# Moving the products of the next key projection ahead of the mixing, a value tile into the second step and half a broadcast one block later, in a two-layer attention kernel

## The chip, the cores and the metric

The kernel runs on one core of one Trainium2 chip. The metric is the device time of one execution in microseconds (us). The kernel before takes 3994.44 us, the median of three runs (3994.28 to 3995.66). All times in this document that carry two decimals and no other mark are read from one profiled execution of the kernel before.

## The reference, cut to what matters

The input x is 8 images of 512 channels and 32 x 32 positions (1024 tokens), in float32. Layer 0 is a group-normalised attention with a projection. Layer 1, where the change lies, is this, for each image, on y, the group-normalised output of layer 0:

```python
q = einsum('oc,bct->bot', w_q, y)      # the same for k and v, 8 heads of 64
attn = einsum('bhdq,bhdT->bhqT', q, k) * scale
attn = einsum('gh,bhqT->bgqT', w_head, attn)     # heads are mixed ahead of the softmax
attn = softmax(attn, axis=-1)
attn = (attn - mean) / sqrt(var + EPS) * gamma + beta   # mean, var over a whole head
out = einsum('bhqT,bhdT->bhqd', attn, v).reshape(b, t, c)
out = out @ w_proj.T + b_proj
```

The result is x plus the output of each layer.

## The kernel before

The engines' instructions stand in the order in which the Python code writes them, engine by engine; a step that is written later is behind all earlier ones on its own engine, and nothing but data and free buffers holds one engine back for another.

Layer 1 goes through the images b = 0 to 7. The queries of an image are cut into eight blocks p = 0 to 7 of 128 queries (NT = 8). A block's work goes through a pipeline of three iterations of p, so the loop has nine iterations p = 0 to 8, each of four steps t = 0 to 3, all in `Attention1.step` (L1852):

- **scores** (L1622, matmul L1629): eight products of keys and queries per block; each goes to a tile of two PSUM banks and is copied to SBUF as `raw`, by ScalarE at L1641 (in the first block every other one by VectorE, L1639).
- **regroup** (L1643, DMA L1647): `raw` is laid out anew by sixteen DMAs of 256 KB per block from SyncE's queue into `re_t`, so that the 8 heads of a query lie in one group of partitions.
- **mix** (L1657, matmul L1666): four mixings of the heads per block, one iteration behind the scores, 32 small matmuls each, into two PSUM tiles; ScalarE takes the exponentials (L1679).
- **flip** (L1687, transpose L1694) and **moments** (L1699, L1708) on VectorE, right behind each mixing.
- **values** (L1712, L1724): attention times v, two iterations behind the scores; ScalarE copies the sums out (**leave**, L1740).
- **totals** (L1756): every second block, three tiny matmuls give the softmax sums of two blocks; their reciprocals go through HBM (four DMAs `zd<-rz`, L1772) and come back spread over the partitions in two DMAs of 256 KB, `rzb<-zd`, L1778. **divide** (L1803) multiplies them into the result, on GpSimd for the first three pairs of blocks. Both the DMAs and the multiplication stand in GpSimd's queue; for the last pair it is SyncE's queue and VectorE.

PSUM tiles of scores, mixings and projections share one pool, `ps_m`, of three buffers of two banks each (L1278, `m_psum`).

An `Agenda` (L28) holds further work under slot numbers; `ag.run(slot)` writes it at that point. `ag.run(4 * p + t)` stands at the end of each step, and some half slots within it. The work in it that matters here:

- `v_pair(b, i)` (L1448): 16 matmuls (L1456) make two of the eight tiles of v; ScalarE copies the first (L1460), VectorE the second (L1461). Pairs 0 and 1 are made between the images, pairs 2 and 3 in slots 1 and 3, that is in the iteration p = 0.
- The key projection of the next image, a `Projection` (L1358) by Strassen-like products in the order 1, 6, 2, 7, 5, 3, 4. `k_go(m)` writes the eight matmuls of product m (L1381) and puts its evacuation on a list, which `k_leave()` (L1443) writes out. Products 1, 2, 6 and 7 have the slots 31.5, 32.5, 33.5 and 34.5, that is the iteration p = 8, which has no scores any more. Product 1 is copied by ScalarE (L1390); product 2 adds to the same bank and is copied by ScalarE (L1435); 6 and 7 are added into partial sums by VectorE (L1396, L1398). `right_y` (L1426, subtractions L1356) makes the right-hand factors on VectorE in slots 32 and 33.
- Loads of the next image and of weights, from SyncE's queue.

In the step, the half slots stand behind the mixing of the step, and `k_leave()` behind those:

```python
                    if old:
                        self.mix(p - 1, 0)
                    ag.run(4 * p - 0.5)
```

Of the kernel before, what the change touches and what calls it, by code (L numbers as in the profile page):

```python
# [467 lines left out]
def tile_two_attention_layers(  # L468
# [19 lines left out]
    nc = tc.nc  # L488
    B, C, T = x_d.shape
    H = w_head.shape[0]  # L490
    D = C // H
# [207 lines left out]
    with ExitStack() as l0:  # L699
# [487 lines left out]
        first = Agenda()  # L1187
# [81 lines left out]
    with ExitStack() as l1:  # L1269
# [15 lines left out]
        def m_psum(nm):  # L1285
            return ps_m.tile([P, 2, FB], F32, tag="m", name=nm)
# [156 lines left out]
        def k_leave():  # L1443
            for fn in due:
                fn()
            due.clear()

        def v_pair(b, i):  # L1448

            if i == 0:  # L1450
                v_t[b] = shared.tile([P, NT, C], F32, tag="v", name=f"v1_{b}")
            ps = m_psum(f"pv1_{b}_{i}")
            w = w_t["v", b]
            for m in range(2):
                for c in range(NCC):
                    nc.tensor.matmul(  # L1456
                        ps[:, m], y_t[b][:, c, ts(2 * i + m, P)], w[:, c],
                        start=(c == 0), stop=(c == NCC - 1),
                    )
            nc.scalar.copy(v_t[b][:, 2 * i], ps[:, 0])  # L1460
            nc.vector.tensor_copy(v_t[b][:, 2 * i + 1], ps[:, 1])  # L1461

        vs = const_tile("vs", [P, H, B])

# [150 lines left out]
        class Attention1:  # L1615
# [140 lines left out]
            def totals(self, n):  # L1756

                b, last = self.b, n == NCH - 1
                bn = self.stats(n)
                del self.bn[n]  # L1760
                ps = acc_psum(f"z1_{b}_{n}")
                nc.tensor.matmul(ps[:64, :32], bn[:, :, 1], sel256, start=True, stop=True)
                for i, x in enumerate((bn[:, :, 2], self.sq)):
                    nc.tensor.matmul(ps[:64, 32:64], x, sel, start=(i == 0), stop=(i == 1))
                rz = stat.tile([64, 32], F32, tag="rz", name=f"rz1_{b}_{n}")
                nc.vector.reciprocal(rz, ps[:64, :32])  # L1766
                nc.vector.tensor_copy(self.zs[:, n], ps[:64, :64])
                zd = dram.tile([2, H, P], F32, tag=f"zd_{b}_{n}", name=f"zd_{b}_{n}")
                queue = nc.sync if last else nc.gpsimd
                for r in range(2):  # L1770
                    for t in range(2):
                        queue.dma_start(  # L1772
                            out=zd[t].rearrange("g (r c q) -> r c g q", r=2, q=4)[r],
                            in_=rz[32 * t + r : 32 * t + 32 : 2].rearrange("c (g q) -> c g q", q=4),
                        )
                self.rzb = zpool.tile([P, T], F32, tag="rzb", name=f"rzb_{b}_{n}")
                for t in range(2):
                    queue.dma_start(  # L1778
                        out=self.rzb[t * D : t * D + D],
                        in_=zd[t].rearrange("g i -> (g i)").partition_broadcast(D),  # L1780
                    )

            def check(self):

# [67 lines left out]
            def step(self, p, t, ag):  # L1852

                new, old, older = p < NT, p >= 1, p >= 2
                if t == 0:
                    if new:
                        for i in range(3):
                            self.scores(p, i)
                    if older:
                        self.values(p - 2, 0, 2, 3)  # L1860
                        self.leave(p - 2, 0)
                        if p % 2:
                            self.sums(p // 2 - 1)
                        if p % 2 == 0 and p >= 4:
                            self.divide(p // 2 - 2, nc.gpsimd)
                    if old:
                        self.mix(p - 1, 0)
                    ag.run(4 * p - 0.5)
                elif t == 1:
                    if older:  # L1870
                        self.values(p - 2, 1, 0)
                        self.flip(p - 1, 0)
                        if p % 2:
                            self.totals(p // 2 - 1)
                        self.moments(p - 1, 0)
                    if new:
                        self.scores(p, 3)
                    if old:
                        self.mix(p - 1, 1)
                    ag.run(4 * p + 0.5)  # L1880
                elif t == 2:
                    if older:
                        self.values(p - 2, 1, 1)
                    if new:
                        self.scores(p, 4)
                        self.scores(p, 5)
                    if old and not new:
                        self.mix(p - 1, 2)
                    ag.run(4 * p + 1.5)
                    if older:  # L1890
                        self.values(p - 2, 1, 2, 3)
                        self.leave(p - 2, 1)
                    if old and new:
                        self.mix(p - 1, 2)
                else:
                    if new:
                        self.scores(p, 6)
                        if old:
                            self.values(p - 1, 0, 0)
                        self.scores(p, 7)  # L1900
                        if old:
                            self.mix(p - 1, 3)
                            self.values(p - 1, 0, 1)
                    else:
                        self.mix(p - 1, 3)
                        self.values(p - 1, 0, 0, 1)
                    ag.run(4 * p + 2.5)
                k_leave()
                if p == 1 or old and t:
                    self.flip(p - 1, t)  # L1910
                    self.moments(p - 1, t)
                if new:
                    for kh, s in (
                        (), ((0, 0), (0, 1), (0, 2)), ((0, 3),), ((1, 0), (1, 1), (1, 2), (1, 3)),
                    )[t]:
                        self.regroup(p, kh, s)
                if old and t == 0:
                    self.piece()
                ag.run(4 * p + t)
# [8 lines left out]
        NV = NT // 4  # L1928
        for b in range(B):
            more = b + 1 < B  # L1930
            a = Attention1(b)
            ag = Agenda()
            for i in range(NV):
                ag.at(1 + 2 * i, lambda i=i: v_pair(b, NV + i))
            if b == 0:
                stages = group_stages(B - 1, B, small_psum1)
                for i in range(3):
# [35 lines left out]
            if not more:  # L1973
                a.values(last, 0, 2, 3)
                a.leave(last, 0)
                a.values(last, 1, 0, 1, 2, 3)
                a.leave(last, 1)
                a.totals(NCH - 1)
                a.instance()
                out1_last(a)  # L1980
                continue
# [4 lines left out]
            a.values(last, 1, 0, 1, 2, 3)  # L1986
            a.leave(last, 1)
            a.totals(NCH - 1)
            a.instance()
            k_leave()  # L1990
            k_go(4, 3)
# [84 lines left out]
```

## Time and profile before

| | us |
|---|---|
| median of three runs | 3994.44 |
| the profiled execution | 3994.71 |
| its span, first to last instruction | 3992.9 |
| TensorE busy with matmuls | 3888.9 |
| VectorE busy | 2772.4 |
| ScalarE busy | 1974.3 |
| GpSimd busy | 141.1 |
| mean granted TensorE clock | 0.994 |

Layer 1 starts at about 1800 us of the span; an image takes about 277 us of it (the first scores of two consecutive images start at 3474.51 and 3751.61).

How to read the lines: PE is TensorE's matmuls, PEld its weight loads, DVE VectorE, ACT ScalarE, POOL GpSimd, SP SyncE. A line of the timeline has start, duration (us), engine, source line, operation, what it writes and reads, shapes, and how many instructions were merged; in brackets is how long the engine sat idle just before, and what ended that. A line of the view of waits has who waited for whom, then the total in us, how often, and the longest. A line of the table by stretches has the stretch, its length, each engine's busy time, and at the end the granted clock of TensorE, the DMA engines' busy share and GB/s.

### The profile page before, as it was taken

Reading aid. Unit: us, or ns where it says so; the run is one execution under the profiler, and the core shown is the slowest. Engines: PE = TensorE matmul, PEld = TensorE weight load, DVE = VectorE, ACT = ScalarE, POOL = GpSimd, SP = SyncE. Lnnn points to the kernel's source line nnn. Section 1 sums busy time; section 2 is a strip of 40 time slices with the busy share of each in tenths; the row PEclk is TensorE's granted clock in tenths of the full one; section 3 lists DMA queues with packets and bytes.
Section 4 is the critical chain, followed back from the end, with each engine's and each line's share of the span. In section 5 each row is a group of like instructions: output and inputs, shape, how many; then the busy total and the mean of one; then the engine's idle time right before and its main releaser. Section 6 shows DMA issues by size and latency. Waiting matters only on the chain. (4 is left out here: it accounts for less than half of the span.)

```text
span 3992.9 us, 95453 instructions
## 1 busy us (share of the span) xinstructions
PE 3888.9 (97%) x41868; PEld 1827.5 (46%) x41868; DVE 2772.4 (69%) x3741; ACT 1974.3 (49%) x2431; POOL 141.1 (4%) x182
## 2 busy tenths in 40 slices
PE   8999999999999999999999999999999999999997
PEld 4353535344343535344544545545444445445354
DVE  4748475766657584856958859859768678588596
ACT  1726363544536271615717628438257166175284
POOL 0000000000000000000100101001001001000010
PEclk9999999999999999999999999999999999999999
DMA  3313131111121221217829749659469287396494
GB/s 121 120 48 117 46 120 48 59 62 67 52 83 57 72 68 58 78 67 186 229 86 229 187 119 242 176 130 232 148 164 229 103 210 205 102 231 183 122 224 122
DMA packets 249593, 519.09 MB, mean 130 GB/s; under 512 B 51024, under 2 KB 58192, under 8 KB 242512
## 3 DMA queue, kind: packets, MB, share of 16 engines
q1 hardware_dynamic: 241984, 500.08, 43.9%
q0 software_dynamic: 7184, 12.81, 1.6%
q8 instruction: 331, 5.42, 0.6%
q14 instruction: 94, 0.77, 0.1%
HBM read 197.16 MB, written 46.92 MB: 61 GB/s over the span
## 5 line engine op out<-in xcount | busy, mean ns | idle before, releaser
L1694 DVE STREAM_TRANSPOSE et<-e 128x2048 f32<-128x2048 f32 x256 | 589.8, 2304 | 155.8 <-ACT e L1679 148.6
L1724 PEld LDWEIGHTS a<-et,v 128*64 128x64 f32 x16384 | 508.0, 138 | 296.2 <-issue 273.2
L1708 DVE BATCH_NORM_STATS2 bn<-e 128x6 f32<-128x512 f32 x1024 | 635.0, 682 | 0.0
L1091 ACT ACTIVATE e<-s 128x1024 f32<-128x1024 f32 x512 | 497.9, 1028 | 233.5 <-PE s L1086 232.2
L1679 ACT ACTIVATE e<-m 128x1024 f32<-128x1024 f32 x512 | 496.9, 1023 | 149.7 <-PE m L1666 51.4
L1724 PE MATMUL a<-et,v 128*64 128x64 f32 x16384 | 555.8, 224 | 13.1 <-DVE et L1694 10.4
L1641 ACT COPY raw<-s 128x1024 f32<-128x1024 f32 x480 | 470.8, 1020 | 183.3 <-PE s L1629 164.5
L1099 DVE TENSOR_TENSOR zacc<-zacc,e 128x1024 f32<-128x1024 f32 x384 | 468.8, 1221 | 84.5 <-ACT e L1091 62.4
L1629 PE MATMUL s<-k,q 64*64 64x512 f32 x4096 | 512.9, 605 | 6.3 <-DVE q L1495 3.1
L1086 PE MATMUL s<-q,k 64*64 64x512 f32 x4096 | 490.1, 593 | 2.3 <-ACT e L1091 2.3
L1112 PE MATMUL a<-e,v 64*64 64x512 f32 x4096 | 484.1, 589 | 0.0
L1666 PE MATMUL m<-re,wmix 32*32 32x512 f32 x8192 | 324.0, 610 | 43.8 <-DMA re<-raw 40.3
L1112 PEld LDWEIGHTS a<-e,v 64*64 64x64 f32 x4096 | 156.7, 133 | 282.8 <-issue 282.2
L1086 PEld LDWEIGHTS s<-q,k 64*64 64x64 f32 x4096 | 147.9, 133 | 275.2 <-issue 240.7
L1629 PEld LDWEIGHTS s<-k,q 64*64 64x64 f32 x4096 | 127.3, 132 | 220.1 <-issue 77.0
L1456 PE MATMUL pv<-wv,y 128*128 128x512 f32 x480 | 212.1, 597 | 0.0
L1740 ACT COPY q<-a 64x256 f32<-64x256 f32 x256 | 94.3, 368 | 190.4 <-PE a L1724 188.7
L1772 POOL DMA_DIRECT2D zd<-rz x96 | 52.5, 552 | 3537.2 <-DVE rz L1766 3535.1
L1666 PEld LDWEIGHTS m<-re,wmix 32*32 32x32 f32 x8192 | 70.8, 103 | 174.2 <-ACT raw L1641 68.6
L1456 PEld LDWEIGHTS pv<-wv,y 128*128 128x128 f32 x480 | 89.3, 190 | 116.9 <-issue 110.3
L1460 ACT COPY v<-pv 128x512 f32<-128x512 f32 x30 | 17.6, 587 | 220.2 <-PE pv L1456 220.2
L1097 DVE TENSOR_TENSOR zacc<-e,e 128x1024 f32<-128x1024 f32 x64 | 78.3, 1224 | 55.5 <-ACT e L1091 55.5
(317 smaller groups left out, 3884.3 us busy)
## 6 DMA issues: line engine op xcount, KB each, us to landing
re<-raw SPq DMA_DIRECT2D x1024, 256.0 KB
left_q<-left_q SPq DMA_DIRECT2D x17, 1792.0 KB
left_p<-left_p SPq DMA_DIRECT2D x17, 1792.0 KB
left_k<-left_k SPq DMA_DIRECT2D x10, 1792.0 KB
x<-in_x_dram SPq DMA_DIRECT2D x32, 512.0 KB
rzb<-zd SPq DMA_DIRECT2D x128, 128.0 KB
x<-x SPq DMA_DIRECT2D x64, 256.0 KB
y<-x SPq DMA_DIRECT2D x32, 512.0 KB
```

Source lines behind the costliest of these rows:

```text
L1086: nc.tensor.matmul(ps[c * D : c * D + D, m], k[r, hp, k0 : k0 + D], q[r, hp, ts(f, FB)], start=True, stop=True,)
L1091: nc.scalar.activation(e[i], ps, AF.Exp, scale=S0 * S0)
L1099: nc.vector.tensor_add(zacc[g], zacc[g], e[i])
L1112: nc.tensor.matmul(acc[g][a][m * D : m * D + D], v[rows, kc, ts(2 * hp + m, D)], e[i][rows, m], start=(kc == 0), stop=(kc == NG - 1),)
L1456: nc.tensor.matmul(ps[:, m], y_t[b][:, c, ts(2 * i + m, P)], w[:, c], start=(c == 0), stop=(c == NCC - 1),)
L1629: nc.tensor.matmul(ps[c * D : c * D + D, m], qo_t[b][r, p, hp, ts(c, D)], k_t[b][r, hp, ts(kh, FB)], start=True, stop=True,)
L1641: nc.scalar.copy(dst, ps)
L1666: nc.tensor.matmul(ps[a // 2][c * 32 : c * 32 + 32, a % 2].rearrange("p (r h k) -> p h r k", r=2, h=2), wmix[rows].rearrange("p g i -> p ( ...
L1679: nc.scalar.activation(e[:, :, 2 * h : 2 * h + 2].rearrange("p r a k -> p a r k"), ps[h].rearrange("p a (r k) -> p a r k", r=2), AF.Exp,)
L1694: nc.vector.transpose(self.et[p, u].rearrange("p kb (r st a) g q -> p st kb r (a g q)", r=2, st=2)[:, st], self.e[p, s].rearrange("p r a ( ...
L1708: nc.vector.bn_stats(self.bn[n][:, p % 2, s, a], e[:, :, a].rearrange("p r k -> p k r"))
L1724: nc.tensor.matmul(acc[two * D : two * D + D, s].rearrange("p (x q) -> p x q", q=4), v_t[b][:, kb, ts(g, D)], et[:, kb, :, g], start=(kb = ...
```

## The change

Six edits, all in layer 1:

1. In every step the half slots, and now `k_leave()` with them, are written ahead of the step's mixing. So each of the products 1, 2, 6 and 7 of the next key projection, and its evacuation, stands ahead of mixing 0, 1, 2 and 3 of the iteration p = 8.
2. A new half slot `4 * p - 0.25` stands behind mixing 0.
3. `v_pair` takes the halves to make. Pair 3 is made in two parts: its first tile in slot 3, as before, its second tile in slot 3.75, that is behind mixing 0 of the iteration p = 1 and ahead of the VectorE work of that step. Each part has a PSUM tile of its own.
4. `broadcast(t)` issues one of the two DMAs `rzb<-zd`. `totals` calls the first; the second is written in step 1 of the next iteration (for the last pair: right behind `totals`).
5. The multiplication on GpSimd, `divide`, moves from step 0 to the end of step 3 of the same iteration.
6. In the first block, all four regroupings of the first half of the keys are written in step 1; before, the fourth was in step 2.

```diff
-        def v_pair(b, i):
+        def v_pair(b, i, ms=range(2)):
...
-            for m in range(2):
+            for m in ms:
...
-            nc.scalar.copy(v_t[b][:, 2 * i], ps[:, 0])
-            nc.vector.tensor_copy(v_t[b][:, 2 * i + 1], ps[:, 1])
+            for m in ms:
+                copy = nc.vector.tensor_copy if m else nc.scalar.copy
+                copy(v_t[b][:, 2 * i + m], ps[:, m])
...
-                for t in range(2):
-                    queue.dma_start(
-                        out=self.rzb[t * D : t * D + D],
-                        in_=zd[t].rearrange("g i -> (g i)").partition_broadcast(D),
-                    )
+                self.zd, self.zq = zd, queue
+                self.broadcast(0)
+
+            def broadcast(self, t):
+
+                self.zq.dma_start(
+                    out=self.rzb[t * D : t * D + D],
+                    in_=self.zd[t].rearrange("g i -> (g i)").partition_broadcast(D),
+                )
...
-                        if p % 2 == 0 and p >= 4:
-                            self.divide(p // 2 - 2, nc.gpsimd)
+                    ag.run(4 * p - 0.5)
+                    k_leave()
                     if old:
                         self.mix(p - 1, 0)
-                    ag.run(4 * p - 0.5)
+                    ag.run(4 * p - 0.25)
                 elif t == 1:
...
                         if p % 2:
                             self.totals(p // 2 - 1)
+                        elif p >= 4:
+                            self.broadcast(1)
                         self.moments(p - 1, 0)
                     if new:
                         self.scores(p, 3)
+                    ag.run(4 * p + 0.5)
+                    k_leave()
                     if old:
                         self.mix(p - 1, 1)
-                    ag.run(4 * p + 0.5)
                 elif t == 2:
...
+                    ag.run(4 * p + 1.5)
+                    k_leave()
                     if old and not new:
                         self.mix(p - 1, 2)
-                    ag.run(4 * p + 1.5)
...
                     else:
+                        ag.run(4 * p + 2.5)
+                        k_leave()
                         self.mix(p - 1, 3)
                         self.values(p - 1, 0, 0, 1)
-                    ag.run(4 * p + 2.5)
-                k_leave()
                 if p == 1 or old and t:
                     self.flip(p - 1, t)
                     self.moments(p - 1, t)
                 if new:
+                    first = 3 + (p == 0)
                     for kh, s in (
-                        (), ((0, 0), (0, 1), (0, 2)), ((0, 3),), ((1, 0), (1, 1), (1, 2), (1, 3)),
+                        [], [(0, i) for i in range(first)], [(0, i) for i in range(first, 4)],
+                        [(1, i) for i in range(4)],
                     )[t]:
                         self.regroup(p, kh, s)
+                if t == 3 and p % 2 == 0 and p >= 4:
+                    self.divide(p // 2 - 2, nc.gpsimd)
...
-            for i in range(NV):
-                ag.at(1 + 2 * i, lambda i=i: v_pair(b, NV + i))
+            ag.at(1, lambda: v_pair(b, NV))
+            ag.at(3, lambda: v_pair(b, NV + 1, [0]))
+            ag.at(3.75, lambda: v_pair(b, NV + 1, [1]))
```

Behind the loop, `a.broadcast(1)` follows `a.totals(NCH - 1)` in both places.

## The prediction

> **What bounds the kernel now.** First I read the page's busy times, then the view of waits of TensorE over layer 1.
>
> ```profile
> PE 3888.9 (97%) x41868; PEld 1827.5 (46%) x41868; DVE 2772.4 (69%) x3741; ACT 1974.3 (49%) x2431; POOL 141.1 (4%) x182
> ```
> ```profile
> PE m L1666 <- DMA re<-raw: 40.3, 22, 4.8
> PE a L1724 <- DVE et L1694: 10.4, 9, 5.3
> ```
>
> TensorE is the bound; only its idle or slowed time can be won. In layer 1 it waits 40.3 us for regrouped scores. The timeline around every mixing that waits places them: 25.34 us lie at mixing 0 of p = 8, once in each of the first seven images (3.52, 4.48, 3.46, 3.60, 3.19, 3.54, 3.55), 4.77 us at the same place of the last image, the other 10.2 us at p = 4, 6 and some others. Then the timeline of TensorE at p = 8 of the seventh image (b = 6), and the table by stretches for the clock:
>
> ```profile
> 3645.95 1.32 PE L1666 MATMUL m<-re,wmix 32*32 32x512 f32 x32 [3.55 <-DMA re<-raw]
> 3647.21 5.18 PE L1381 MATMUL pk<-y,left_k 128*128 128x512 f32 x8
> 3652.32 1.15 PE L1724 MATMUL a<-et,v 128*64 128x64 f32 x32
> 3653.40 1.14 PE L1666 MATMUL m<-re,wmix 32*32 32x512 f32 x32
> 3654.47 3.70 PE L1381 MATMUL pk<-y,left_k 128*128 128x512 f32 x8
> 3658.10 1.15 PE L1724 MATMUL a<-et,v 128*64 128x64 f32 x32
> ```
> ```profile
> 3646.80:3650.20 3.40, 3.40 (x20) 1.45 (x5) 3.13 (x3) 1.94 (x2) 0.00 (x0) 0.50 1.09 285
> ```
>
> After the wait the clock is halved (0.50) for 3.4 us. Mixing plus product, start to start, take 4.70 us at full clock (3653.40 to 3658.10) and 6.37 here: 1.67 lost. The same sum is 6.37 or 6.36 in four other images and 7.38 and 7.67 in the two whose halved stretch is 6.8 us, so 14.0 us in seven images. The first place thus holds 25.34 + 14.0 = 39.3 us.
>
> The second place is p = 1 of every image, TensorE and VectorE:
>
> ```profile
> 3499.25 1.59 PE L1666 MATMUL m<-re,wmix 32*32 32x512 f32 x32
> 3502.03 2.06 PE L1666 MATMUL m<-re,wmix 32*32 32x512 f32 x32 [0.18 <-ACT e L1679]
> 3506.30 1.94 PE L1666 MATMUL m<-re,wmix 32*32 32x512 f32 x32
> 3509.89 1.15 PE L1724 MATMUL a<-et,v 128*64 128x64 f32 x32 [0.63 <-DVE et L1694]
> ```
> ```profile
> 3502.93 2.31 DVE L1694 STREAM_TRANSPOSE et<-e 128x2048 f32<-128x2048 f32 x1 [5.00 <-ACT e L1679]
> 3505.16 2.47 DVE L1708 BATCH_NORM_STATS2 bn<-e 128x6 f32<-128x512 f32 x4
> 3507.55 2.29 DVE L1694 STREAM_TRANSPOSE et<-e 128x2048 f32<-128x2048 f32 x1
> ```
>
> From mixing 0 to the first values pass 10.64 us, while TensorE has three mixings (1.07 each) and four scores (0.86 each), 6.7 us. So 4 us are lost, mostly inside mixings that stand with one bank missing. What ends it is VectorE: flip 0, moments, flip 1.
>
> **What the skill says.** The Trainium skill, "TensorE: Matmul & The Clock Gate", Part 1: the clock is granted by activity in free-running windows of 3413 ns, full or half. The trace agrees (0.50 for 3.4 or 6.8 us). Its section on architectural detail calls ScalarE, VectorE and GpSimd strict FIFO; the trace agrees below. "Trainium Kernel Development and Optimization", Key Constraints: the queues of SP, ACT and POOL share 16 DMA engines. The trace agrees: from 3639.3 to 3646.0, with GpSimd's broadcasts under way, the DMA share is 1.05.
>
> **Part A: products ahead of the mixing (b = 0 to 6).** Count from T0 = 3642.40, the end of the values ahead of mixing 0 (3645.95 - 3.55). A product takes 3.63 from start to start (3654.47 to 3658.10), values x32 1.08.
>
> Product 1 runs 0 to 3.63. Its inputs and bank are ready: the last raw copy ended at 3639.42. Data for mixing 0 are there at 3.55, so it starts at 3.63 without waiting, at full clock. Only the second image keeps 4.48 - 3.63 = 0.85. Then: mixing 0 to 4.70, values to 5.78, product 2 to 9.41, mixing 1 to 10.48, values to 11.56, product 6 to 15.19, mixing 2 to 16.26, values x64 to 18.28.
>
> Banks: in the trace, mixing 2 starts at 3659.18 while the copy of product 2's bank still runs (3658.21 to 3659.22), so it holds others. I infer that a new tile takes the buffer released longest ago in program order. Then mixings 1, 2 and 3 take the pair that the exponentials of the mixing before freed, and products 6, 7 and 5 follow one another in the third buffer. ScalarE waits for products 1 and 2 with the exponentials behind; these need later mixings anyway.
>
> The catch is VectorE. Product 7 needs product 6's bank, freed by the addition L1396, and behind `right_y`. VectorE's order: flip and moments of block 6, `right_y`, flip 0, moments 0, flip 1, moments 1, `right_y`, addition. Flip 0 waits for the exponentials: mixing 0 at 3.63, first exponential 1.34 later (3653.40 to 3654.74), both 1.94, so 6.91. Flip and moments start 4.61 apart (3642.02 to 3646.62). Mixing 1 at 9.41 gives flip 1 at 12.72, `right_y` at 17.33, the addition at 19.67 (`right_y` takes 2.34: 1.12 from its first subtraction at 3661.36 to the second, and 1.22), done at 20.89. With 0.16 for the hand-over (as the 0.18 in the lines above) product 7 starts at 21.05: TensorE stands 21.05 - 18.28 = **2.77 us**, and mixing 3, values x64 and product 5 stand behind it. Before, mixing 3 and two values filled this time.
>
> Then product 7 to 24.68, mixing 3 to 25.76, values to 27.80, product 5 to 31.43. Before, the values that follow product 5 start at 3676.05 = T0 + 33.65. Gain 2.2 us in this image. For the others I add the difference of their own wait and slow clock to 5.22: 3.2, 2.3 (after its 0.85), 2.1, 2.3, 1.9, 3.5, 2.2, together **17.5 us**.
>
> Does the clock halve again after 2.77 us? Against free-running windows, it does if some 2.0 us or more fall in one window (estimate: waits of 1.0 to 1.5 halved nothing, 3.19 did): (3.41 - 2.77 + 2 x 0.77) / 3.41, or some 0.6 of the phases. Cost 1.7 x 7 x 0.6 = 7.1; bounds 0 and 7 x 2.9 = 20. A brings 17.5 - 7.1 = **10.4 us**.
>
> **Part B: second tile of pair 3 in p = 1 (all eight).** Removed from p = 0: eight matmuls, 3.43 us, so all up to mixing 0 comes 3.43 earlier, at 3495.82. Its data should then be there: the regroupings can start once the last raw copy ends (VectorE, 3490.81), and two DMAs of 256 KB take 1.9 us at the 270 GB/s of the saturated stretch 3639.3 to 3646.0; with some 2 us from issue to first data (an estimate, half of the 4.0 that the page of DMA issues gives for the small `zd<-rz`) that is 3495. The eight matmuls follow at 3497.33 and end at 3501.06 (3496.62 - 3489.45 = 7.17 for sixteen, less 3.44). VectorE's copy (0.69) stands **ahead of flip 0** in its queue, so flip 0, ready at 3499.5, starts at 3501.75, not 3502.93. The 3.43 us fill the hole but hold back the chain that makes it; values come 1.18 us earlier: 8 x 1.18 = **9.4 us**. The fourth regrouping of p = 0 is one step earlier on SP's queue, with nothing between that waits: 0. If data come 1.2 us later than estimated, B is 0.
>
> **Part C: broadcast and divide.** GpSimd's own timeline:
>
> ```profile
> 3552.08 0.54 POOL L1778 DMA_DIRECT2D rzb<-zd  x1 [3.95 <-DMA re<-raw]
> 3552.81 0.52 POOL L1778 DMA_DIRECT2D rzb<-zd  x1 [0.19 <-issue]
> 3559.91 2.35 POOL L1805 TENSOR_TENSOR q<-q,rzb 128x1024 f32<-128x1024 f32 x1 [6.58 <-ACT raw L1641]
> ```
>
> The second broadcast is written a block later, but on GpSimd nothing stands between the two: its 182 instructions are these, the zd writes, the divides and the constants. Its data are the same, so it still goes out some 0.2 us after the first, and the divide still follows as soon as both land. C: **0**.
>
> **Sum.** 10.4 + 9.4 = 19.8 us. The profiled execution took 3994.71 (span 3992.9 and 1.8 around it), 0.27 above the median; 3994.44 - 19.8 = **3974.6 us**.
>
> **Rivals.**
> - *The broadcast does move* (its issue would have to be held by TensorE's or VectorE's progress; the lines above speak against it). Each odd block then loses one DMA of 256 KB, about 1 us: nearly all of the 10.2 us, 0.85, and 1 of the last image's 4.77 go: 3974.6 - 12 = **3963**. Chance 0.12.
> - *Product 7 gets a bank of mixing 2.* Then it runs at 18.28 and covers the addition: no 2.77 us, no halved clock: 17.5 + 19.4 + 9.4 = 46, **3948**. The bank order speaks against it. Chance 0.10.
> - *Slower: mixing 2 gets product 6's bank.* Then it stands from 15.19 until the addition at 21.0, 5.8 us, with a halved clock of some 2.8 as after the longest waits: A = 36.9 - 7 x 8.6 = -23, with B -14 in all: **4008**. It is slower once wait and slow clock pass (36.9 + 9.4) / 7 = 6.6 us per image. The start at 3659.18 speaks against it. Chance 0.10.
> - The forecast, 0.68.
>
> Range 3955.5 (the first rival with no halved clock: 7.1 less) to 3988 (halved every time at 2.2 us, so A = 2.1, and half of B); 0.2 lie outside. A measurement of this kernel tells about 0.2%, 8 us, from no change. Faster by more: 0.68 + 0.12 + 0.10, less 0.06 for the forecast's weak end: 0.84; within 0.06; slower 0.10.
>
> **What would show it.** No wait for regroupings at mixing 0 of p = 8 in the first seven images; a new wait of some 2.8 us at the fourth product, ended by L1396; flip 0 of p = 1 right behind a VectorE copy of v; the two broadcasts still back to back. Wrong if product 7 doesn't wait, if mixing 2 does, or if broadcasts lie 10 us apart.

## The result and the profile after

The changed kernel takes 3964.74 us, the median of six runs (3963.44 to 3966.52), against 3994.69 for the kernel before beside it: ratio 0.9926, 95% interval 0.9913 to 0.9938, 30 us less. The forecast was 3974.6, so the time is 9.9 us below it and inside its range. All times below that carry two decimals and no other mark are from one profiled execution of the kernel named; that of the changed kernel took 3964.89.

In the changed kernel the numbering moves by one to five lines: scores L1630, copies of raw L1640 and L1642, mixing L1667, exponentials L1680, transpose of the flip L1695, moments L1709, values L1725, broadcast L1783, division L1810, copy of v L1462. The lines of the projection (L1356, L1381, L1396, L1398) stay. The products of the key projection run in the order 1, 2, 6, 7, 5, 4, 3; the order 1, 6, 2, ... given with the kernel before is that of the query projection.

The busy times first, then the view of waits of TensorE over layer 1 (who waited for whom, total in us, how often, longest):

```profile
PE 3874.9 (98%) x41868; PEld 1823.7 (46%) x41868; DVE 2769.6 (70%) x3741; ACT 1971.4 (50%) x2431; POOL 141.2 (4%) x182
```
```profile
PE m L1667 <- DMA re<-raw: 16.5, 15, 3.8
PE pk L1381 <- DVE re L1398: 8.2, 7, 1.2
PE a L1725 <- DVE et L1695: 7.8, 9, 5.3
...
PE pk L1381 <- DVE right L1356: 2.6, 7, 0.4
```

The waits for regroupings fall from 40.3 to 16.5 us. Two new ones appear, each once in each of the first seven images. Both stand in TensorE's timeline at p = 8 of the seventh image (b = 6):

```profile
3619.20 3.70 PE L1381 MATMUL pk<-y,left_k 128*128 128x512 f32 x8
3622.83 1.14 PE L1667 MATMUL m<-re,wmix 32*32 32x512 f32 x32
...
3635.47 2.08 PE L1725 MATMUL a<-et,v 128*64 128x64 f32 x64
3637.91 3.67 PE L1381 MATMUL pk<-right,left_k 128*128 128x512 f32 x8 [0.36 <-DVE right L1356]
3641.52 1.14 PE L1667 MATMUL m<-re,wmix 32*32 32x512 f32 x32
...
3645.84 3.70 PE L1381 MATMUL pk<-right,left_k 128*128 128x512 f32 x8 [1.17 <-DVE re L1398]
3649.47 5.82 PE L1725 MATMUL a<-et,v 128*64 128x64 f32 x192
```

The values ahead of product 1 end at T0 = 3619.27 (the ends are modelled, so the product's start, 3619.20, lies a little earlier), and mixing 0 follows the product without a wait and at full clock. Product 7 waits 0.36 us for its right-hand factor, product 5 waits 1.17. From T0 to the values behind product 5 pass 30.20 us; it was 33.65 before. VectorE in the same stretch shows which buffer product 7 has:

```profile
3637.69 1.22 DVE L1356 TENSOR_TENSOR right<-y,right 128x1024 f32<-128x1024 f32 x1
3638.82 1.21 DVE L1396 TENSOR_TENSOR re<-re,pk 128x1024 f32<-128x1024 f32 x1
...
3644.59 1.19 DVE L1398 TENSOR_TENSOR re<-re,pk 128x1024 f32<-128x1024 f32 x1
```

L1396 is the addition that empties product 6's buffer. It begins at 3638.82, 0.9 us *after* product 7 has begun, so product 7 does not stand in that buffer. The pool has three buffers; mixing 2, which started at 3634.39 while product 6 still held one, had the other two, so product 7 has one of these. Product 5 waits for L1398, the addition of product 7, so product 5 stands in product 7's.

At p = 1 of the same image, TensorE and then VectorE:

```profile
3475.49 3.70 PE L1456 MATMUL pv<-wv,y 128*128 128x512 f32 x8
...
3486.80 1.15 PE L1725 MATMUL a<-et,v 128*64 128x64 f32 x32 [0.31 <-DVE et L1695]
```
```profile
3479.23 0.69 DVE L1462 COPY v<-pv 128x512 f32<-128x512 f32 x1 [10.26 <-PE pv L1456]
3479.84 2.30 DVE L1695 STREAM_TRANSPOSE et<-e 128x2048 f32<-128x2048 f32 x1
```

The second v tile now fills TensorE behind mixing 0, and flip 0 begins as VectorE's copy of it ends. From an image's first scores to its first values pass 34.12 us, before 35.39, in every image but the first.

GpSimd's timeline shows that the second broadcast did not move (in layer 1 the two start within 3 us of each other every time):

```profile
3528.07 0.54 POOL L1783 DMA_DIRECT2D rzb<-zd  x1 [3.39 <-DMA re<-raw]
3528.95 0.52 POOL L1783 DMA_DIRECT2D rzb<-zd  x1 [0.33 <-issue]
```

Set out by place, with the same sums taken from both profiled executions:

| place | forecast | measured |
|---|---|---|
| p = 8 of seven images, T0 to the values behind product 5 (238.35 to 212.52) | -10.4 | -25.8 |
| first scores to first values, eight images (291.6 to 282.9) | -9.4 | -8.7 |
| wait at p = 8 of the last image (4.77 to 3.82) | 0 | -0.95 |
| waits ahead of mixing 0 of p = 4 and 6 (11.2 to 13.8) | 0 | +2.6 |
| other idle time of the values (2.7 to 3.4) | 0 | +0.7 |
| halved clock at 1939.0 and 3034.7, 1.7 each | 0 | +3.4 |
| sum | -19.8 | -28.8 |

The waits at p = 4 and 6 include those whose last releaser in the profile is ScalarE's copy of raw, so they don't sum to the lines of the view of waits. The two executions differ by 29.8; 1.0 us of it is not placed. The forecast was too small at one place, p = 8.

### The profile page after: what moved, and what is told of

The parts are those of the page before. It is cut to its first block, busy times and chain, and to the rows that moved or that the text cites. A ratio compares the mean times of both kernels' runs of the same rounds, so it can differ in the third digit from the quotient of the medians.

```text
span 3963.1 us, 95453 instructions
## 1 busy us (share of the span) xinstructions
PE 3874.9 (98%) x41868; PEld 1823.7 (46%) x41868; DVE 2769.6 (70%) x3741; ACT 1971.4 (50%) x2431; POOL 141.2 (4%) x182
## 3 DMA queue, kind: packets, MB, share of 16 engines
q8 instruction: 331, 5.42, 0.6%
## 4 chain that ended last, share of the span: by engine, by line
PE 90%; DVE 5%; DMA 3%; ACT 1%; issue 1%; SPq 0%; ACTq 0%; DVEq 0%
PE s L1086 11%; PE a L1112 11%; PE a L1725 11%; PE s L1630 10%; PE m L1667 6%; PE pk_p L904 6%; PE pq_p L904 5%; PE pv L1456 5%; PE pv_p L904 5%; PE pp_p L904 5%; PE pq L1381 4%; PE pp L1381 4%; PE pk L1381 3%; DMA re<-raw 3%; DVE et L1695 1%; DVE bn L1709 1%
## 5 line engine op out<-in xcount | busy, mean ns | idle before, releaser
L1695 DVE STREAM_TRANSPOSE et<-e 128x2048 f32<-128x2048 f32 x256 | 589.5, 2303 | 100.0 <-ACT e L1680 99.0
L1725 PEld LDWEIGHTS a<-et,v 128*64 128x64 f32 x16384 | 510.8, 139 | 296.4 <-issue 273.4
L1709 DVE BATCH_NORM_STATS2 bn<-e 128x6 f32<-128x512 f32 x1024 | 635.1, 681 | 0.0
L1642 ACT COPY raw<-s 128x1024 f32<-128x1024 f32 x480 | 470.2, 1018 | 211.6 <-PE s L1630 179.0
L1680 ACT ACTIVATE e<-m 128x1024 f32<-128x1024 f32 x512 | 496.3, 1021 | 156.1 <-issue 56.3
L1725 PE MATMUL a<-et,v 128*64 128x64 f32 x16384 | 558.9, 225 | 11.2 <-DVE et L1695 7.8
L1630 PE MATMUL s<-k,q 64*64 64x512 f32 x4096 | 515.2, 607 | 5.8 <-DVE q L1496 3.2
L1667 PE MATMUL m<-re,wmix 32*32 32x512 f32 x8192 | 311.0, 602 | 19.5 <-DMA re<-raw 16.5
L1630 PEld LDWEIGHTS s<-k,q 64*64 64x64 f32 x4096 | 127.8, 132 | 220.8 <-issue 87.1
L1456 PE MATMUL pv<-wv,y 128*128 128x512 f32 x480 | 214.3, 599 | 0.0
L1667 PEld LDWEIGHTS m<-re,wmix 32*32 32x32 f32 x8192 | 68.8, 103 | 162.4 <-ACT raw L1642 69.3
L1462 DVE COPY v<-pv 128x512 f32<-128x512 f32 x30 | 20.7, 689 | 159.5 <-PE pv L1456 80.9
```

Of the source, the lines that this page charges most:

```text
L1456: nc.tensor.matmul(ps[:, m], y_t[b][:, c, ts(2 * i + m, P)], w[:, c], start=(c == 0), stop=(c == NCC - 1),)
L1630: nc.tensor.matmul(ps[c * D : c * D + D, m], qo_t[b][r, p, hp, ts(c, D)], k_t[b][r, hp, ts(kh, FB)], start=True, stop=True,)
L1642: nc.scalar.copy(dst, ps)
L1667: nc.tensor.matmul(ps[a // 2][c * 32 : c * 32 + 32, a % 2].rearrange("p (r h k) -> p h r k", r=2, h=2), wmix[rows].rearrange("p g i -> p ( ...
L1680: nc.scalar.activation(e[:, :, 2 * h : 2 * h + 2].rearrange("p r a k -> p a r k"), ps[h].rearrange("p a (r k) -> p a r k", r=2), AF.Exp,)
L1695: nc.vector.transpose(self.et[p, u].rearrange("p kb (r st a) g q -> p st kb r (a g q)", r=2, st=2)[:, st], self.e[p, s].rearrange("p r a ( ...
```

## The experiments

Twelve kernels ran, in three groups of four, each group on one chip beside the kernel before, which took 3999.06, 4001.08 and 3998.89 us there and scattered by 9 to 20 us. Ratios are to the kernel before of the own group. An interval is some 3 to 8 us wide to each side, so differences of a few us are read at their place in the trace.

| kernel | median us | ratio | 95% interval |
|---|---|---|---|
| a_only | 3971.24 | 0.9927 | 0.9915 to 0.9940 |
| b_only | 3987.15 | 0.9972 | 0.9961 to 0.9983 |
| c_only | 3999.99 | 1.0003 | 0.9994 to 1.0011 |
| k7_same_bank | 3977.43 | 0.9944 | 0.9929 to 0.9958 |
| after_again | 3963.53 | 0.9901 | 0.9882 to 0.9920 |
| ab_no_c | 3966.96 | 0.9911 | 0.9893 to 0.9929 |
| bcast_sync | 3947.99 | 0.9864 | 0.9843 to 0.9884 |
| bcast_sync_both | 3957.87 | 0.9890 | 0.9869 to 0.9910 |
| first_only | 3958.32 | 0.9898 | 0.9883 to 0.9913 |
| vector_order | 3953.53 | 0.9891 | 0.9875 to 0.9906 |
| v_scalar | 3960.12 | 0.9900 | 0.9885 to 0.9915 |
| all_three | 3937.64 | 0.9842 | 0.9828 to 0.9855 |

The theory after the result was: the mechanisms of parts A, B and C are as forecast, and only the inferred buffer of product 7 was wrong. Its rivals: A's gain is of another kind than covering mixing 0, or the broadcast did something after all.

**One part at a time.** a_only is the kernel before with the first edit:

```diff
+                    ag.run(4 * p - 0.5)
+                    k_leave()
                     if old:
                         self.mix(p - 1, 0)
-                    ag.run(4 * p - 0.5)
```

and the same in steps 1 to 3.

> Only the half slots and the writing out of the evacuations go ahead of the mixing (the first edit); v tile, broadcast, divide and regroupings stay as before. Theory: this part is worth what the trace of the changed kernel shows between the end of the values ahead of mixing 0 of p = 8 and the values behind product 5, 30.3 us against 33.7 before: 7 x 3.4 and the larger waits of two images, some 26 us, so about 3968 us, ratio 0.9934, and no halved clock at p = 8. Rival, the forecast's own size: 10.4 us, about 3984 us, ratio 0.9974.

Measured: 0.9927, 29 us. The interval leaves the forecast's 0.9974 out. In its trace the seven stretches from T0 sum to 214.3 us (before 238.35, so 24 us less), none at halved clock. The theory holds.

b_only is the kernel before with the v tile in two parts (edits 2 and 3, and 6 with them):

```diff
-            for i in range(NV):
-                ag.at(1 + 2 * i, lambda i=i: v_pair(b, NV + i))
+            ag.at(1, lambda: v_pair(b, NV))
+            ag.at(3, lambda: v_pair(b, NV + 1, [0]))
+            ag.at(3.75, lambda: v_pair(b, NV + 1, [1]))
```

> Only pair 3 of v is made in two parts, the second behind mixing 0 of p = 1, and the fourth regrouping of the first block goes to step 1; everything else as before. Theory: 1.2 us in each of eight images, some 10 us, about 3984.5 us, ratio 0.9975, and flip 0 of p = 1 right behind VectorE's copy of v. Rival: the gain of p = 1 is taken back in the same image by the next wait for regroupings, so less than 3 us (ratio 0.9993 or more), and most of the change's gain belongs to the first edit.

Measured: 0.9972, 11 us. First scores to first values take 34.12 or 34.11 us in seven images and 42.62 in the first (before 35.38 or 35.39 and 43.90): 8 x 1.27 = 10.2 us. The wait at p = 8 stays (30.4 us over eight images, before 30.1), so nothing is taken back there.

c_only is the kernel before with edits 4 and 5:

```diff
-                for t in range(2):
-                    queue.dma_start(
-                        out=self.rzb[t * D : t * D + D],
-                        in_=zd[t].rearrange("g i -> (g i)").partition_broadcast(D),
-                    )
+                self.zd, self.zq = zd, queue
+                self.broadcast(0)
...
-                        if p % 2 == 0 and p >= 4:
-                            self.divide(p // 2 - 2, nc.gpsimd)
...
+                        elif p >= 4:
+                            self.broadcast(1)
```

> Only the second broadcast and the division are written later (edits 4 and 5). Theory: GpSimd has nothing between the two broadcasts, so both go out back to back as before: ratio 1.000 within 0.001, same DMA waits as before. Rival 1: the broadcast is spread and the waits for regroupings at even blocks shrink by 10 us, ratio 0.9975. Rival 2: this part is what makes the waits at even blocks of the changed kernel 2 to 3 us longer, ratio 1.0006.

Measured: 1.0003. Both broadcasts still go out together, within 3 us. The waits at p = 4 and 6 are 12.8 us against 11.2 before; in a_only and b_only they are 13.9 and 13.0, so the part with the broadcast isn't what lengthens them. They differ by a few us from kernel to kernel, and I have no cause for that.

after_again is the changed kernel itself, beside three variants.

> The changed kernel itself, beside the other kernels of this group on one chip, so that the parts (0.9927 for the first edit alone, 0.9972 for the v tile alone, 1.0003 for broadcast and division alone) can be set against the whole. Theory: the parts add up, less 2 to 3 us of longer waits for regroupings, ratio 0.991 to 0.992. Rival: whole and first edit alone are the same, 0.9927, because the gain of the v tile is given back by later waits when both stand together.

Measured: 0.9901. The product of the three parts is 0.9927 x 0.9972 x 1.0003 = 0.9902: they add up. The rival (whole equal to the first edit alone) would give 0.9927, outside this interval; but the first measurement of the same kernel gave 0.9926, which the rival fits. The ratios alone don't decide. The traces do: in both profiled executions of the changed kernel the values come after 34.12 us, as in b_only, and the seven stretches sum to 212.5 and 215.9, as in a_only. ab_no_c then leaves the broadcast and the division as before:

```diff
...
-                        elif p >= 4:
-                            self.broadcast(1)
...
```

> The changed kernel with the broadcasts and the division written as before (edits 1, 2, 3 and 6 without 4 and 5). Theory: broadcast and division do nothing, ratio to the changed kernel 1.000 within 0.001. Rival: they cost the 2 to 3 us of longer waits at even blocks, or more, and without them the time is 3 to 8 us less than that of the changed kernel.

Measured: 0.9911 beside 0.9901, each inside the other's interval, with the median 3 us on the side of *no* gain from leaving C out. C is worth nothing that can be seen.

**The buffer of product 7.** k7_same_bank puts the changed kernel into the state that the forecast had inferred, products 6, 7 and 5 in one buffer one after another:

```diff
+                elif m == 7 and self.nm[:3] == "pk1" and self.nm != "pk1_0":
+                    self.ps[7] = self.six
                 else:
                     self.ps[m] = m_psum(f"{self.nm}_{m}")
+                    if m == 6:
+                        self.six = self.ps[6]
```

> The changed kernel, but product 7 is written into product 6's own PSUM tile, so that the buffers stand as the forecast inferred them (products 6, 7 and 5 in one buffer one after another). Theory (the forecast failed only in this inference): product 7 waits 2.3 to 2.8 us for VectorE's addition into which product 6 goes, and product 5 then no longer waits its 1.2 us, so about 1.1 us per image, 8 us in all if the clock isn't halved, about 3973 us, ratio to the changed kernel 1.002; with the halved clock in 6 of 10 images 15 us, about 3980 us. Rival: the buffer doesn't matter, the wait of 0.36 us for the right-hand factor stays and the time is that of the changed kernel within 2 us.

Measured: 0.9944; against 0.9902, the product of the parts of its own group, that is 0.0042 or 17 us slower. The view of waits and the timeline of the sixth image (four lines further down in this kernel, L1400 is the addition L1396), then the table by stretches for the clock:

```profile
PE pk L1385 <- DVE re L1400: 17.8, 7, 2.5
```
```profile
3376.60 2.08 PE L1729 MATMUL a<-et,v 128*64 128x64 f32 x64
3381.22 5.40 PE L1385 MATMUL pk<-right,left_k 128*128 128x512 f32 x8 [2.54 <-DVE re L1400]
```
```profile
3382.00:3385.40 3.40, 3.40 (x5) 1.35 (x4) 3.40 (x5) 0.00 (x0) 0.00 (x0) 0.50 0.00 0
```

Product 7 waits 2.54 us for the addition, in all seven images, and product 5 no longer waits. In five of the seven images the clock is then halved for 3.4 us, and product 7 takes longer, in this one 5.40 us instead of 3.67. The seven stretches sum to 228.15 us. The forecast's value for part A meant 238.35 - 10.4 = 227.95. So its working was right for the buffers it assumed, and the buffer alone makes 228.15 - 212.52 = 15.6 us. (Beside the other execution of the changed kernel, 215.9, it is 12.3; the difference is mostly that one's longer waits at mixing 0.)

**Which product has to be ahead.** first_only leaves product 1 ahead of mixing 0 and puts 2, 6 and 7 back behind their mixings:

```diff
+                    if old:
+                        self.mix(p - 1, 1)
                     ag.run(4 * p + 0.5)
                     k_leave()
-                    if old:
-                        self.mix(p - 1, 1)
...
```

and products 6 and 7 likewise, with their evacuations at the end of the step.

> The changed kernel with product 1 alone ahead of its mixing; products 2, 6 and 7 go back behind mixings 1, 2 and 3. Theory: only the wait at mixing 0 had to be covered, and the other three products bring nothing of the gain and the new waits of 0.36 and 1.17 us per image; from T0, the end of the values ahead of mixing 0, to the values behind product 5 pass 28.4 us (33.65 before less the 5.22 of wait and slow clock) and up to 1.3 more where mixing 1 now comes too early for its buffers, against 30.2 in the changed kernel: 3 to 12 us less than the changed kernel. Rival: the products have to be ahead one and all, since mixings 1 to 3 meet waits of their own without them: longer than 30.2 us per image.

Measured: 0.9898; the seven stretches sum to 210.1 us, 2.4 less than in the changed kernel. The shortest of them, those without a wait for data at mixing 0, take 29.54 against 30.20, which over seven images is 4.6. Both new waits of the products are gone, and another has come, in the timeline at mixing 1:

```profile
3618.07 2.05 PE L1667 MATMUL m<-re,wmix 32*32 32x512 f32 x32 [0.17 <-ACT e L1680]
```

It waits for a buffer from the exponentials and runs 2.05 instead of 1.14 us. All of A's gain is product 1 ahead of mixing 0. The other three moves cost 0.7 us per image, in the lower part of what was expected. This holds with VectorE's order as it is in the changed kernel: in the next experiment, with all four products ahead and another order, a stretch takes 28.56. Product 1 alone with that order was not run.

**VectorE's order at p = 8.** vector_order puts the factors ahead of moments 1, and the addition of product 7 ahead of moments 2:

```diff
                         k_leave()
+                        self.moments(p - 1, 2)
                         self.mix(p - 1, 3)
...
                     self.flip(p - 1, t)
-                    self.moments(p - 1, t)
+                    if t == 1 and not new:
+                        ag.run(4 * p + t)
+                    if t != 2 or new:
+                        self.moments(p - 1, t)
```

> The changed kernel with VectorE's order in p = 8 changed: the second half of the right-hand factors goes ahead of moments 1, and the addition of product 7 goes ahead of moments 2. Theory: both new waits (0.36 at product 7, 1.17 at product 5) come from VectorE's queue and go, 28.7 us from T0 to the values behind product 5, 7 x 1.53 = 10.7 us less than the changed kernel, ratio to it 0.9973. Rival: flips come later by as much, and values behind them take the wait over: same time as the changed kernel.

VectorE's timeline:

```profile
3617.63 1.18 DVE L1356 TENSOR_TENSOR right<-y 128x1024 f32<-128x1024 f32 x1
...
3625.65 1.17 DVE L1398 TENSOR_TENSOR re<-re,pk 128x1024 f32<-128x1024 f32 x1
3626.76 2.49 DVE L1709 BATCH_NORM_STATS2 bn<-e 128x6 f32<-128x512 f32 x4
```

The addition L1398 now stands right behind the flip and ahead of the moments. Both waits are gone in all seven images, a stretch takes 28.56 us (28.7 expected), and the sum is 200.8, which is 11.7 less than in the changed kernel. No later values wait in their place. The ratio, 0.9891, is 4 to 14 us better than the changed kernel's two (0.9901 and 0.9926), which were taken in other groups; the trace carries the verdict.

**The copy of v.** v_scalar gives the second v tile's copy to ScalarE:

```diff
-                copy = nc.vector.tensor_copy if m else nc.scalar.copy
+                copy = nc.vector.tensor_copy if m and len(ms) == 2 else nc.scalar.copy
```

> The changed kernel with the second v tile of pair 3 copied by ScalarE, so that it no longer stands ahead of flip 0 on VectorE. Theory (the forecast's step for the v tile: the chain copy, flip 0, moments, flip 1 sets when the first values start): flip 0 follows the exponentials some 2 us earlier and the last wait of 0.3 us ahead of the values goes, after which TensorE's own work and ScalarE's copies set the pace: 0.3 to 1 us per image, 2.5 to 8 us in all, ratio to the changed kernel 0.998 to 0.9994. Rival: ScalarE's copy delays the exponentials of mixing 1 and the time is the same or more.

```profile
3478.08 2.31 DVE L1695 STREAM_TRANSPOSE et<-e 128x2048 f32<-128x2048 f32 x1 [8.68 <-ACT e L1680]
3480.31 2.48 DVE L1709 BATCH_NORM_STATS2 bn<-e 128x6 f32<-128x512 f32 x4
3483.83 2.31 DVE L1695 STREAM_TRANSPOSE et<-e 128x2048 f32<-128x2048 f32 x1 [1.04 <-ACT e L1680]
```

Flip 0 now follows the exponentials, and the wait of 0.31 ahead of the values is gone in all eight images. First scores to first values take 33.74 us in seven images, 0.38 less: over eight images 3.0 us. The chain copy, flip, moments, flip was what set the first values; once it is shorter by two us, flip 1 waits for the exponentials of mixing 1 and TensorE's own work sets the pace. The ratio, 0.9900, can't show 3 us, and longer waits at p = 4 and 6 in this execution (16.1 us) hide them.

**The broadcast made to move.** bcast_sync issues the second broadcast from SyncE's queue:

```diff
-                self.zq.dma_start(
+                queue = nc.sync if t else self.zq
+                queue.dma_start(
```

> The changed kernel with the second broadcast issued from SyncE's queue at the place where it is written, so that it really goes out a block later (the forecast's first rival made true; the first broadcast stays in GpSimd's queue). Theory of the rival, from the forecast: each odd block loses 256 KB at the crowded time, about 1 us, so the waits for regroupings at p = 4 and 6 shrink from 12.7 us to some 4 and the last image's wait at p = 8 from 3.8 to 2.8, about 9 us less than the changed kernel, ratio to it 0.998. Against it: the transfers that delay the regroupings are the regroupings themselves, and the waits stay, ratio 1.000.

Measured: 0.9864 beside 0.9901, 15.5 us less than the changed kernel. SyncE's queue at p = 4 of the second image, and then the view of waits:

```profile
2150.04 15.56 SPq L1648 DMA_DIRECT2D re<-raw  x13
2165.64 0.89 SPq L1339 DMA_DIRECT2D y<-x  x1
2166.64 0.60 SPq L1784 DMA_DIRECT2D rzb<-zd  x1
```
```profile
PE m L1667 <- DMA re<-raw: 3.6, 4, 2.9
```

The first broadcast goes out at 2155.43, the second at 2166.64, behind the regroupings that mixing 0 (at 2164.09) needs. The waits at p = 4 and 6 fall from 13.5 us (after_again) to 0.4, and the last image's wait at p = 8 from 4.47 to 2.94, and the waits at the same place of the first seven images, 3.7 us in after_again, are gone. The other broadcast of 256 KB still runs beside the regroupings, and yet no wait is left. The waits at even blocks thus come from the second broadcast as GpSimd's queue issued it. The Trainium skill, "Trainium Kernel Development and Optimization", Key Constraints, says that the queues of the issuing engines share 16 DMA engines and interleave; this agrees. The second broadcast also changed its kind of queue (from software to hardware dynamic in the view of the DMA queues); time and queue weren't separated, so that its being under way at that time is the cause is likely and not shown.

bcast_sync_both moves the first broadcast as well:

```diff
-                self.broadcast(0)
+                if last:
+                    self.broadcast(0)
...
                         elif p >= 4:
+                            self.broadcast(0)
                             self.broadcast(1)
```

with SyncE's queue for all of them.

> As the last, with both broadcasts of the first three pairs issued from SyncE's queue a block later, so that no broadcast is under way while the second half of an odd block is regrouped. Rival of the forecast: twice the effect, about 2 us per odd block: waits at p = 4 and 6 nearly gone, last image's wait 1.8 us, 12 to 14 us less than the changed kernel, ratio to it 0.9967. If the waits stay, broadcasts are not what they come from.

Measured: 0.9890, *less* than with one moved. The waits ahead of mixing 0 of p = 4 and 6 are gone here too (0.3 us), and the last image's at p = 8 falls to 1.94. But the other mixings, scores and values of p = 3 to 7 now wait 11 us against some 5 in bcast_sync, most of it with no releaser in the profile. Six of the first seven images take 0.4 to 8.1 us longer than in bcast_sync. Of the 13.4 us between the two profiled spans (3959.7 and 3946.3) I can put only these 6 down to waits; by place, 8.1 lie in the third image alone and 2.3 ahead of layer 1, where the two kernels are the same. Why the expected 12 to 14 us did not come stays open.

**Together.** all_three is bcast_sync, vector_order and v_scalar in one kernel.

> The changed kernel with the second broadcast in SyncE's queue, VectorE's order in p = 8 as in vector_order, and the second v tile copied by ScalarE. Theory: the gains lie at different places and add up, 15 + 10.7 + 2.5, some 28 us less than the changed kernel, ratio to it 0.993, about 0.983 to the kernel before. Rival: less DMA waiting moves the regroupings so that other waits take up the difference, 15 us or less.

Measured: 3937.64 us, 0.9842, 61 us less than the kernel before and 23 to 34 us less than the changed kernel (by its ratios 0.9901 and 0.9926). Waits for regroupings are 5.1 us, the seven stretches at p = 8 sum to 201.6, first scores to first values take 33.74 us. The gains add up, as far as the ratios can tell.

## Why the forecast was right in direction and too small

- **What bounds the kernel** was read rightly: all of the gain came from waits and slow clock of TensorE, at the two places named.
- **Part A, the first wait:** right. Mixing 0 follows product 1 with no wait over 0.2 us in six of the seven images (0.71 us in one), and the clock isn't halved there in any. In after_again, the same kernel, four images wait 0.28 to 1.72 us there: the data come at times that differ between executions, and one product doesn't cover all of it. first_only shows that moving product 1 alone brings A's whole gain.
- **Part A, the buffers:** this step failed. The forecast inferred that "products 6, 7 and 5 follow one another in the third buffer". Product 7 got a buffer of mixing 2 instead, the rival given 0.10. The forecast's ground, that a new tile takes the buffer released longest ago in program order, doesn't hold; which rule the placement follows stays open.
- **Part A, VectorE's time:** right. The addition of product 6 was forecast to be done 20.89 us after T0 and is done after 20.76. With product 7 in product 6's buffer the wait is 2.54 us (forecast 2.77) and the clock is halved in five of seven images (forecast 0.6 of the phases). 228.15 us was measured where 227.95 was forecast; that they agree to 0.2 is partly luck, since the wait was 1.6 us shorter over seven images and the halved clock, at 1.7 per stretch, 1.4 us more.
- **Part A, what was not forecast:** with its own buffer, product 7 starts early and waits 0.36 us for its factor, and product 5 then waits 1.17 us for the addition of product 7. The 2.77 us and the halved clock (7.1 us) of the forecast became 1.53 us and none. The rival had set no wait at all and 36.9 us for A; it came out 11.1 too high, which is the 7 x 1.53 = 10.7 us.
- **Part B:** right in mechanism and size, 9.4 us forecast, 10.2 in the part by itself; 8.7 in the whole, since a stretch of halved clock fell into the first image.
- **Part C:** right at 0. The price that the first rival set on a broadcast that does move, 9 to 12 us, was a little low: 15.5.
- **Left out:** waits at even blocks, other idle time and halved clock elsewhere grew by 6.7 us. One of these stretches, at 1939.0, follows a wait of 1.98 us at 1938.04. Part of the rest is scatter between executions: the waits at p = 4 and 6 are 11.6 us in first_only and 16.1 in v_scalar, with the same broadcasts. The two errors, 15.4 us too little at p = 8 and 6.7 us of losses left out, partly cancelled, and so the time lies nearer to the forecast than its steps do.

**The clock.** The halved clock agrees with the Trainium skill, "TensorE: Matmul & The Clock Gate", Part 1, which lets free-running windows of 3413 ns decide: in each of the fourteen profiled executions all switches of the clock lie on one grid of that step, to 0.01 us. So the same wait can do either thing: the 2.54 us of k7_same_bank was followed by a halved stretch in five images and by none in two. Two windows of that grid from its trace, each with the one behind it (behind the comma stands TensorE's busy time; the clock is the third number from the end):

```profile
3378.56:3381.97 3.41, 0.87 (x8) 0.49 (x3) 3.41 (x4) 0.91 (x3) 0.00 (x0) 1.00 0.00 0
3381.97:3385.38 3.41, 3.41 (x5) 1.35 (x4) 3.41 (x5) 0.00 (x0) 0.00 (x0) 0.50 0.00 0
2549.12:2552.53 3.41, 1.66 (x4) 0.87 (x5) 3.41 (x3) 0.00 (x0) 0.00 (x0) 1.00 0.00 0
2552.53:2555.94 3.41, 3.41 (x49) 1.18 (x49) 3.41 (x6) 0.10 (x1) 0.00 (x0) 1.00 0.00 0
```

In the first image shown the whole wait falls into one window and the next is halved; in the second the wait is split, 1.75 us in its fuller window, and the next is not. The measurement differs from that page in how much idle time it takes: there, the half clock comes back after at least one idle window. Here, over the fourteen traces from 1835 to 3850 us, each cut on its own grid, all 31 full-speed windows in which TensorE is idle for 1.92 us or more are followed by a halved one, 2 of the 6 between 1.74 and 1.91, and none of the more than 8000 below. The forecast's estimate of some 2.0 us was near. A halved window is followed by another halved one in all 7 cases in which TensorE is idle for 0.47 us or more in it, and by a full one in all 33 with 0.24 or less; that makes the stretches of 6.8 and of 3.4 us. Ahead of 1835 us there is an exception, here in the changed kernel:

```profile
1822.28 3.90 PE L1474 MATMUL pvs<-ys,wv 128*64 128x8 f32 x128
```

These small matmuls of eight columns leave TensorE no idle time in the profile, and yet the window behind them is halved in 11 of the 14 traces. So the profile's busy time isn't quite what decides.

## What to carry to other kernels

An independent piece of work that stands just behind a wait is worth moving ahead of it when the engine's slow clock after the wait is counted too: here one product of 3.6 us per image took 39 us of waits and slow clock away, of which some 13 came back, 10.7 of them as later waits for VectorE. Who owns which buffer decides whether such a move pays: read it from the trace (does the writer start before the old reader has begun?), and carry both cases as numbers until then. A DMA that is only written later isn't issued later if its queue has nothing to hold it; check the issue times. Here it went out later once it stood in a queue behind the transfers that it was not to disturb.

## What the runs showed of the hardware that was not expected

Some idle stretches of TensorE have no releaser in the profile ("issue"). They can lie within one group of matmuls, as in this mixing of bcast_sync, which stands still after 28 of its 32:

```profile
3578.05 1.16 PE L1667 MATMUL m<-re,wmix 32*32 32x512 f32 x28
3580.71 1.05 PE L1667 MATMUL m<-re,wmix 32*32 32x512 f32 x4 [1.50 <-issue]
```

In four executions (the changed kernel, bcast_sync, bcast_sync_both, v_scalar) all 20 such gaps of more than 0.4 us in layer 1 end 1.3 to 2.1 us after a packet of the DMA kind "instruction" has landed on queue 8; over all fourteen traces it is 40 of 43. About one tenth of the time lies that far behind such a packet, so chance would give 4. The packets have 16,384 bytes each (331 of them, 5.42 MB), and in layer 1 one comes per 256 instructions of TensorE in the mean, some seven in 60 us. So TensorE may wait there for its own instructions, which come through the same DMA engines as the data; then something other than data and free buffers holds an engine back. No run was made to test this. In bcast_sync_both these gaps sum to 8.1 us, in bcast_sync to 4.5.
